# Block sums turned by VectorE instead of TensorE in a two-layer graph kernel, with another order of layer 0's loads and last work

## The chip, the cores and the metric

One core of a Trainium2 chip runs the kernel. The metric is the device time of one execution in microseconds (us). The five engines of the core are called by the profile's names: PE (TensorE; PEld is its weight load), DVE (VectorE), ACT (ScalarE), POOL (GpSimd) and SP (SyncE, which here only issues DMAs; SPq is its queue).

## The reference, cut to what matters

A graph with 3327 nodes and 128 features goes through two layers. Layer 0 is a graph convolution with batch norm; layer 1 is attention with 128 heads of width 8, whose logits get the adjacency matrix added twice.

```python
# layer 0
h = relu(layernorm(x))
deg = adj.sum(axis=1); deg = where(deg == 0, 1, deg)
agg = adj.T @ h / deg
h = agg @ W_n.T + b_n + h @ W_c.T + b_c
x = x + relu(gamma * (h - mean(h)) * rsqrt(var(h) + 1e-5) + beta)   # over nodes
# layer 1
h = relu(layernorm(x))
q, k, v = ((h @ W.T).reshape(128, 3327, 8) for W in (Wq, Wk, Wv))
a = einsum('dnh,dmh->dnm', q, k) * 128 ** -0.5 + adj + adj
out = einsum('dnm,dmh->dnh', softmax(a), v)
x = x + out.reshape(3327, 1024) @ Wo.T
```

## The kernel before, in words

All of it is one stream for each engine, in the order in which the program issues it; each engine works its stream in order, and waits where a tile that it needs isn't ready or a buffer isn't free.

**Layer 0** (from line 301). Nodes come in 26 chunks of 128. The features `xs` and all weights are loaded by DMAs on ACT's queue (L325 to L337), the adjacency rows `a`, one chunk of 1.66 MB after the other, on SP's (L431), with three buffers. `stats` and `normalise` (L345, L363) make the layer norm of all chunks ahead of the chunk loop. In the loop PE multiplies each chunk into seven banks `acc` (L433, 14 matmul records a chunk), ACT sums the rows of `a` (L437), DVE takes their largest value (L440), and `beside` and `spread` fit smaller matmuls in between: A turned, A times W_c, the norms of the weights, and the reciprocal degrees spread over partitions. Then `hidden` and the loop at L504 finish the convolution and its batch norm, with the last two `spread`s, `set_flag` (a bound that tells whether the plain exponentials are safe) and `weigh_early` in between. L570 to L617 make the residual, the second layer norm and its columns, project head group 0 to q, k, v, and write these and the columns `hd` to DRAM. SP and ACT load k, q and v back (L587 to L597), and POOL and ACT sort k's columns (L613).

**Attention** (from line 675). Heads are taken four at a time: 32 groups `i`, and in each the queries in 7 blocks `y` of `QB` = 476 columns (the last has 472), and in each block the 26 key chunks in 13 steps `s`. So there are 32 x 7 x 13 = 2912 steps. A step has four products (`product`, L750: two matmuls of 32 rows into one of three PSUM buffers). Three of them go through DVE, which adds the adjacency (`add`, L862), and then ACT takes one exponential of all three (`late`, L907). The fourth goes to ACT first (L871) and then to POOL, which multiplies it by exponentials of the adjacency that were made once and lie in DRAM (`weighted`, L874). In steps 3, 7 and 11 (`DOUBLE`) it is two and two. Three steps later (`LAG`) PE multiplies the exponentials by v, with a column of ones, into the block's bank `av` (`second`, `weigh`, L623): for each of the four heads, at partitions 32b to 32b + 8, eight sums and the divisor. Two banks take turns by block.

**The end of a block** (`finish`, L628) is a generator whose parts run inside the next block's steps, one part at each step in `PARTS` = 3, 5, 6, 7, 8. Step 3: DVE copies the sums to SBUF (L633). Steps 5 and 6: PE turns them, four matmuls of two records each against the identity, two in each step (L640), back into the bank. Step 7: DVE clamps and inverts the divisors and multiplies (L648, L649, L651). Step 8: SP stores the quotients to `att` (L658; L665 for the last rows). Into steps 7 and 11 the program also fits the projections of later head groups and the output product of the group before (`begin`, `go_on`; L208, L269, L279). SP loads the adjacency tiles `at` (four buffers) and the exponentials `wt` (three) two steps ahead (`fetch`, L734, L738), and q, k, v of the next group spread evenly over a group's steps (`loads`). q is loaded in four DMAs of 8 rows for each head and k in two of 16 rows, since each half of q and the whole of k stand twice in their 32 rows (L140, L148).

Of the kernel before, what the change touches and what calls it, by code (L numbers as in the profile page):

```python
# [20 lines left out]
H = 8  # L21
# [5 lines left out]
QB = 476  # L27
# [9 lines left out]
PARTS = (3, 5, 6, 7, 8)  # L37
# [9 lines left out]
def tile_two_layer_gnn(  # L47
# [42 lines left out]
    xd = dram.tile([NP, D], F32, name="xd")  # L90
# [47 lines left out]
    def q_loads(q, p0, d, n0=0, n=NP):  # L138

        qs = qT[:, bass.ds(d * N + n0, n)].rearrange("(a h) n -> a h n", h=H)  # L140
        return [
            (q[p0 + i * H : p0 + (i + 1) * H, n0 : n0 + n].bitcast(F32), qs[i // 2])
            for i in range(4)
        ]

    def k_loads(k, p0, d, n0, n):
        cols = bass.ds(d * N + n0, n)
        return [  # L148
            (k[p0 + i * 2 * H : p0 + (i + 1) * 2 * H].bitcast(F32), kT[:, cols])
            for i in range(2)  # L150
        ]
# [52 lines left out]
    def projection(wk, hj, j, s, e, quick, ov, factor):  # L204
# [8 lines left out]
        if s == 2:  # L213
# [5 lines left out]
            if e:  # L219
                nc.sync.dma_start(  # L220
# [3 lines left out]
        o = wk.tile([P, 2, NB], F32R, name="o")  # L224
        factor = 1.0 if s else factor
        if quick:
            nc.scalar.activation(o[:CH, 0], bank[:CH], AF.Copy, scale=factor)
            nc.vector.scalar_tensor_tensor(
                o[:CH, 1], bank[:CH], factor, o[:CH, 0].bitcast(F32), ALU.mult, ALU.subtract
            )  # L230
        else:
# [3 lines left out]
            else:  # L235
# [3 lines left out]
                o[:CH, 1], f[:CH], o[:CH, 0].bitcast(F32), ALU.subtract  # L239
            )  # L240
        yield
        for a in range(2):
            g = a * H + e * (H // 2)
            nc.sync.dma_start(
                (qT, kT)[s][g : g + H // 2, tok].rearrange("g (p u) -> p g u", u=D),
                o[:CH, a].bitcast(F32).rearrange("p (h u) -> p h u", u=D),
            )

    def projections(wk, hj, j, quick, ov, factor):
        return [  # L250
            projection(wk, hj, j, s, e, quick, ov, factor) for s in (1, 0, 2) for e in range(2)
        ]

    def outputs(wk, j):
# [7 lines left out]
        nc.sync.dma_start(xj[:CH], xd[j * CH : (j + 1) * CH, :])  # L262
# [38 lines left out]
    with tc.tile_pool(name="l0", bufs=1) as l0, tc.tile_pool(  # L301
        name="l0adj", bufs=3
    ) as ap, tc.tile_pool(name="l0s", bufs=2) as sp, tc.tile_pool(
# [18 lines left out]

        xr = x[: (NC - 1) * P, :].rearrange("(c p) d -> p c d", p=P)
        nc.vector.memset(xs[:, NC - 1, :], 0.0)
        for c0, c1 in ((0, 8), (8, NC - 1)):  # L325
            nc.scalar.dma_start(xs[:, c0:c1, :], xr[:, c0:c1, :])
        for p0, p1 in pieces(N - (NC - 1) * P):
            nc.scalar.dma_start(
                xs[p0:p1, NC - 1, :], x[(NC - 1) * P + p0 : (NC - 1) * P + p1, :]
            )  # L330
        nc.scalar.dma_start(wc, WcT)
        for i, b in enumerate((b_n, b_c, gamma, beta)):
            nc.scalar.dma_start(cols[:, i : i + 1], b.rearrange("o d -> d o"))
        nc.scalar.dma_start(wn, WnT)
        for t, w in zip(wqk, (WqT, WkT, WvT)):
# [781 lines left out]
```

## Time and profile before

| | |
|---|---|
| median of 3 runs | 10376.06 us (10374.61 to 10379.81) |
| the profiled execution | 10381.98 us, span of its instructions 10380.2 us |
| first adjacency matmul | 23.45 us after the start |
| first product of the attention (L750) | 261.67 us |
| first addition by DVE (L862) | 271.80 us |
| one head group in the middle | 313 us, 7 blocks |
| last exponential begins | 10353.66 us |
| TensorE clock granted, mean | 0.992 |

The attention is 97% of the time, and it repeats 32 times; what a step in it costs is multiplied by 2912, and what a block costs by 224. Busy shares in this profile are read with care: a matmul's end is modelled, so that PE seems busy while its result waits. The starts of ACT's instructions, one after another, tell more: an engine that begins the next instruction as soon as the one before it lets it isn't waiting. In an answer on time, a row is "start, duration, engine, line, operation, what is written and read, shape, count", and brackets at the end tell how long the engine stood idle before it and what ended that.

### The profile page before, as it was taken

How to read it: one execution, taken by the hardware profiler on the slowest of the kernel's cores; microseconds unless marked ns; L12 is line 12 of the kernel's file. 1: busy time of each engine (PE TensorE's matmuls, PEld its weight loads, DVE VectorE, ACT ScalarE, POOL GpSimd, SP SyncE). 2: the span in 40 equal slices, each digit the busy share in tenths (PEclk: the TensorE clock that was granted, in tenths of full speed). 3: DMA queues.
4: the chain of work that ended last, by engine and by line, in shares of the span. 5: the costliest groups of instructions: out<-in, count | busy, mean ns of one | idle time of the engine just before them, and what ended most of it. 6: DMA issues, size and time to landing. Idle time of an engine off the chain costs nothing. (4 is left out here: it accounts for less than half of the span.)

```text
span 10380.2 us, 189900 instructions
## 1 busy us (share of the span) xinstructions
PE 9995.3 (96%) x73327; PEld 3082.3 (30%) x73327; DVE 9366.9 (90%) x9533; ACT 9923.2 (96%) x6655; POOL 8439.0 (81%) x4317
## 2 busy tenths in 40 slices
PE   7899999999999999999999999999999999999999
PEld 3222222222222222222222222222222222222222
DVE  5789999999999999999999999999999999999998
ACT  4899999999999999999999999999999999999998
POOL 1678888888888888888888888888888888888887
PEclk9899999999999999999999999999999999999999
DMA  6766666666666666666665666666666665666554
GB/s 228 221 177 164 163 170 167 166 165 165 163 166 170 165 165 162 164 168 167 167 164 159 168 167 168 167 161 162 167 169 167 167 161 159 171 169 167 157 153 127
DMA packets 1114449, 1735.99 MB, mean 167 GB/s; under 512 B 194622, under 2 KB 1089980, under 8 KB 1105852
## 3 DMA queue, kind: packets, MB, share of 16 engines
q1 hardware_dynamic: 1108766, 1716.94, 60.9%
q8 instruction: 575, 9.42, 0.4%
q10 hardware_dynamic: 4350, 4.20, 0.1%
q14 instruction: 342, 2.80, 0.1%
q0 software_dynamic: 416, 2.63, 0.1%
HBM read 1621.05 MB, written 102.38 MB: 166 GB/s over the span
## 5 line engine op out<-in xcount | busy, mean ns | idle before, releaser
L862 DVE SCALAR_TENSOR_TENSOR d<-at,s 128x952 f32<-128x952 f32 x8064 | 8797.4, 1141 | 681.7 <-PE s L750 397.6
L874 POOL TENSOR_TENSOR f<-f,wt 128x952 f32<-128x952 f32 (+1 forms) x3584 | 7939.0, 2233 | 1674.3 <-ACT f L871 1649.9
L907 ACT ACTIVATE d<-d 128x2856 f32<-128x2856 f32 (+1 forms) x2912 | 7027.9, 2413 | 2.2 <-DVE d L862 1.9
L623 PE MATMUL av<-d,v 128*9 128x476 f32 x32256 | 5065.6, 566 | 0.7 <-ACT d L907 0.7
L750 PE MATMUL s<-q,k 32*128 32x476 f32 x23296 | 4087.3, 475 | 313.8 <-ACT f L871 243.5
L871 ACT ACTIVATE f<-s 128x952 f32<-128x952 f32 (+1 forms) x3584 | 3396.9, 970 | 281.8 <-PE s L750 266.0
L750 PEld LDWEIGHTS s<-q,k 32*128 32x128 f32 x23296 | 1739.5, 182 | 5500.2 <-DVE d L862 3005.9
L623 PE MATMUL av<-f,v 128*9 128x476 f32 x14336 | 2849.0, 566 | 0.0
L623 PEld LDWEIGHTS av<-d,v 128*9 128x9 f32 x32256 | 583.3, 88 | 1161.5 <-issue 1149.6
L640 PE MATMUL av<-ident,avs 128*119 128x36 f32 (+1 forms) x1792 | 474.1, 391 | 0.8 <-DVE avs L633 0.8
L640 PEld LDWEIGHTS av<-ident,avs 128*119 128x119 f32 (+1 forms) x1792 | 422.9, 308 | 103.1 <-issue 101.5
L623 PEld LDWEIGHTS av<-f,v 128*9 128x9 f32 x14336 | 316.6, 88 | 112.4 <-issue 88.7
L192 POOL CAST k<-ks 128x256 fp32r<-128x256 f32 x434 | 283.8, 654 | 0.0
L433 PE MATMUL acc<-a,A 128*128 128x512 f32 (+1 forms) x364 | 151.6, 569 | 24.2 <-ACT A L367 23.4
L238 POOL TENSOR_TENSOR o<-pf,o 104x512 fp32r<-104x512 f32 x124 | 160.0, 1291 | 9.9
L633 DVE COPY avs<-av 128x476 f32<-128x476 f32 (+1 forms) x224 | 145.4, 649 | 4.6 <-PE av L623 4.6
L440 DVE TENSOR_REDUCE amax<-a 128x1 f32<-128x3327 f32 x26 | 93.7, 3611 | 36.4 <-DMA a<-in_adj 36.4
L433 PEld LDWEIGHTS acc<-a,A 128*128 128x128 f32 x364 | 69.0, 192 | 109.0 <-issue 84.5
L236 DVE TENSOR_SCALAR pf<-av,low_half 104x512 f32<-104x512 f32 x62 | 46.6, 751 | 46.8 <-PE av L208 46.6
L406 POOL TENSOR_TENSOR sq<-wk 128x512 f32<-128x512 f32 x2 | 2.1, 1042 | 102.5 <-PE aside L407 102.5
L234 DVE COPY pf<-av 104x512 f32<-104x512 f32 x62 | 42.9, 692 | 46.9 <-PE av L208 46.9
L437 ACT ACTIVATE junk<-a 128x3327 bf16<-128x3327 f32 x26 | 77.5, 2979 | 7.1 <-DMA a<-in_adj 6.8
(123 smaller groups left out, 1032.3 us busy)
## 6 DMA issues: line engine op xcount, KB each, us to landing
at<-in_adjT SPq DMA_DIRECT2D x1728, 476.0 KB
wt<-wd SPq DMA_DIRECT2D x1536, 238.0 KB
at<-in_adjT SPq DMA_DIRECT2D x288, 472.0 KB
wt<-wd SPq DMA_DIRECT2D x256, 236.0 KB
ks<-kT SPq DMA_DIRECT2D x496, 104.0 KB
q<-qT SPq DMA_DIRECT2D x496, 104.0 KB
a<-in_adj SPq DMA_DIRECT2D x26, 1663.5 KB
kT<-o SPq DMA_DIRECT2D x128, 208.0 KB
```

What stands on the lines that cost most here:

```text
L192: nc.gpsimd.tensor_copy(k[:, c : c + n, half * 64 : half * 64 + 64], ks.bitcast(F32).rearrange("g (p c) -> g c p", c=NC)[:, c : c + n, :],)
L238: nc.gpsimd.tensor_tensor(o[:CH, 1], f[:CH], o[:CH, 0].bitcast(F32), ALU.subtract)
L433: nc.tensor.matmul(acc[i][:, :w], A[:, c, :], a[:, n0 : n0 + w], start=(c == 0), stop=(c == NC - 1),)
L440: nc.vector.tensor_reduce(amax[:, c : c + 1], a[:, :N], AX.X, ALU.max, apply_absolute_value=True)
L623: nc.tensor.matmul(av[32 * b : 32 * b + H + 1, :w], tiles[2][:, b, c, :], e, start=first, stop=last,)
L633: nc.vector.tensor_copy(avs[:, : R * J], av[:, : R * J])
L640: nc.tensor.matmul(pt[:R, j, :], avs[:, j : j + (R - 1) * J + 1 : J], some, start=True, stop=True)
L750: nc.tensor.matmul(p[:, x, :we], k[rs, c, :], q[rs, n0 : n0 + we], start=True, stop=True,)
L862: nc.vector.scalar_tensor_tensor(d[:, j, :, :w], have[0, i, y, c // 2][:, c % 2, :w] .unsqueeze(1).to_broadcast([P, 2, w]), SAFE / 2, p[:, ...
L871: nc.scalar.activation(f[:, :, :w], p[:, :, :w], AF.Exp, scale=2.0)
L874: nc.gpsimd.tensor_tensor(f[:, :, :w], f[:, :, :w], have[1, i, y, c][:, :w].unsqueeze(1).to_broadcast([P, 2, w]), ALU.mult,)
L907: nc.scalar.activation(flat, flat, AF.Exp, scale=2.0)
```

## The change

- `finish`: DVE turns the sums itself, in 32 x 32 squares, reading the bank and writing `avs` in SBUF; the four matmuls go. The block is taken as 32 runs of J columns (15, or 14 in the last block), so `QB` becomes 480 and the last block 448, and 32 J is the block's width. The reciprocals are written into J spare columns of the block's bank, from column 480. `PARTS` loses steps 5 and 6. The store to `att` is one DMA for each of the four heads, 32 rows of 480 bytes, and in the last block of a group two for each.
- q and k loads: one DMA for what stood in two, with the source repeated by a stride of zero: q two DMAs for each head, k one. Half as many are issued.
- Layer 0: the features come on SP's queue, the first four chunks ahead of the first adjacency chunk and the rest between the next ones; q, k, v and output weights follow between later chunks; small weights move to POOL's queue; ACT takes its square root once at the start. The layer norm is made chunk group by chunk group in the chunk loop. In the last chunk the flag and the last `spread` are made between the matmuls.
- From layer 0 to the attention: projections of group 0 are spread over the residual work, with their stores on three queues; `hd` is written in two parts, `xd` once in another layout (read back in one or two DMAs); the first loads of k, q, v and the sorting of k move into the attention, behind its first `at` and `wt` loads, all on SP; the pools of the attention are laid out in another order.

```diff
-QB = 476
+QB = 480
-PARTS = (3, 5, 6, 7, 8)
+PARTS = (3, 7, 8)
-            (q[p0 + i * H : p0 + (i + 1) * H, n0 : n0 + n].bitcast(F32), qs[i // 2])
-            for i in range(4)
+            (
+                q[p0 + a * 2 * H : p0 + (a + 1) * 2 * H, n0 : n0 + n].bitcast(F32),
+                qs[a].unsqueeze(0).to_broadcast([2, H, n]),
+            )
+            for a in range(2)
         ]
     def k_loads(k, p0, d, n0, n):
-        cols = bass.ds(d * N + n0, n)
-        return [
-            (k[p0 + i * 2 * H : p0 + (i + 1) * 2 * H].bitcast(F32), kT[:, cols])
-            for i in range(2)
-        ]
+        ks = kT[:, bass.ds(d * N + n0, n)]
+        return [(
+            k[p0 : p0 + 4 * H].bitcast(F32), ks.unsqueeze(0).to_broadcast([2, 2 * H, n])
+        )]
...
-        nc.sync.dma_start(xj[:CH], xd[j * CH : (j + 1) * CH, :])
+        for c in range(j * CH // P, ((j + 1) * CH - 1) // P + 1):
+            m0, m1 = max(j * CH, c * P), min((j + 1) * CH, (c + 1) * P)
+            nc.sync.dma_start(
+                xj[m0 - j * CH : m1 - j * CH], xd[m0 - c * P : m1 - c * P, c, :]
+            )
...
+        nc.sync.dma_start(xs[:, :4, :], xr[:, :4, :])
+        tiles = []
+
+        def load(c):
+
+            a = ap.tile([P, 7 * NB], F32, name="a")
+            nc.sync.dma_start(a[:, :N], adj[c * P : (c + 1) * P, :])
+            tiles.append(a)
+            if c in (1, 2):
+                c0, c1 = (4, 14) if c == 1 else (14, NC - 1)
+                nc.sync.dma_start(xs[:, c0:c1, :], xr[:, c0:c1, :])
+            if c == 2:
+                for p0, p1 in pieces(N - (NC - 1) * P):
+                    nc.sync.dma_start(
+                        xs[p0:p1, NC - 1, :], x[(NC - 1) * P + p0 : (NC - 1) * P + p1, :]
+                    )
+            if c in (5, 7, 9):
+                i = (c - 5) // 2
+                nc.sync.dma_start(wqk[i], (WqT, WkT, WvT)[i])
+            if c == 11:
+                nc.sync.dma_start(wo, WoT.rearrange("(e p) o -> p e o", p=P))
+
+
+        root = l0.tile([P, 1], F32, name="root")
+        nc.scalar.activation(root, eps, AF.Sqrt)
+        nc.gpsimd.dma_start(wc, WcT)
         for i, b in enumerate((b_n, b_c, gamma, beta)):
-            nc.scalar.dma_start(cols[:, i : i + 1], b.rearrange("o d -> d o"))
-        nc.scalar.dma_start(wn, WnT)
-        for t, w in zip(wqk, (WqT, WkT, WvT)):
-            nc.scalar.dma_start(t, w)
-        nc.scalar.dma_start(wo, WoT.rearrange("(e p) o -> p e o", p=P))
+            nc.gpsimd.dma_start(cols[:, i : i + 1], b.rearrange("o d -> d o"))
+        nc.gpsimd.dma_start(wn, WnT)
...
-        stats(0)
-        for i in range(NQ):
-            if i + 1 < NQ:
-                stats(i + 1)
-            normalise(i, A)
-        nc.vector.tensor_add(bias, cols[:, 0:1], cols[:, 1:2])
...
+        load(0)
+        for c in range(NC):
+            a = tiles[c]
+            if c + 1 < NC:
+                load(c + 1)
+            if c < NQ:
+                if c == 0:
+                    stats(c)
+                normalise(c, A)
+                if c + 1 < NQ:
+                    stats(c + 1)
+
+            def gather(i0, i1):
+                for i, (n0, w) in list(enumerate(blocks))[i0:i1]:
+                    nc.tensor.matmul(
+                        acc[i][:, :w], A[:, c, :], a[:, n0 : n0 + w],
+                        start=(c == 0), stop=(c == NC - 1),
+                    )
+
+            last = c == NC - 1
+            gather(0, 4 if last else len(blocks))
+            nc.scalar.activation(
+                junk, a[:, :N], AF.Copy, accum_out=deg[:, c : c + 1]
+            )
+            nc.vector.tensor_reduce(
+                amax[:, c : c + 1], a[:, :N], AX.X, ALU.max, apply_absolute_value=True
+            )
+            if last:
+                nc.vector.tensor_reduce(top, amax, AX.X, ALU.max)
+                flags = set_flag()
+                next(flags)
+                gather(4, len(blocks))
+                next(flags)
+                spreading = spread(NQ - 1)
+                next(spreading)
+            if c >= 1:
+                beside(c - 1)
+            if c - 1 == 2 * NQ + 4:
+                set_bound()
+
+            i = c - 2 * NQ - 5
+            if 0 <= i < NQ - 1 and 4 * i + 4 <= c:
+                for _ in spread(i):
+                    pass
...
@@ -507,11 +560,9 @@
             nc.tensor.matmul(acc[i][:, :w], wn, B2[:, s], start=True, stop=True)
             if i >= 1:
                 hidden(i - 1)
-            if i in (0, 2):
-                spread(NQ - 2 + i // 2)
-            if i == 3:
-                set_flag()
-            if i in (4, 6):
+            if i == 0:
+                next(spreading)
+            if i in (0, 1):
                 weigh_early()
...
+        now = projections(
+            sp, B2[:, :CH], 0, True, ov, low_half[:CH, 1:2], (nc.scalar, nc.sync, nc.gpsimd)
+        )
+        banks = [acc[i] for i in (6, 5, 4, 0)] + [aside, acc[1]]
+
+        def multiply(*js):
+            for j in js:
+                drive(now[j], banks[j])
+
+        def project(*js):
+            for j in js:
+                drive(now[j])
+                drive(now[j])
+
+        multiply(0, 1)
+        project(0, 1)
         residual(2)
-        project_now(0, [acc[j] for j in (6, 5, 4, 0)] + [aside, acc[1]])
-
-        q, k, v = sets[0]
-        ks = sets[1][1].rearrange("p c n -> p (c n)")
-        for b in range(G):
-            for args in k_loads(ks, 32 * b, b, 0, NP):
-                nc.sync.dma_start(*args)
-        for args in v_loads(v, 0):
-            nc.sync.dma_start(*args)
+        multiply(2, 3)
+        relu(4)
+        stats(2, False)
+        project(2, 3)
+        residual(3)
+        multiply(4, 5)
+        relu(5)
+        stats(3, False)
+        relu(6)
+        project(4, 5)
         for i in range(4, NQ):
-            relu(i)
-
-        for b in range(G):
-            for args in q_loads(q, 32 * b, b, 0, NB):
-                nc.scalar.dma_start(*args)
-        for i in range(2, NQ):
-            if i > 2:
...
     def finish(rp, av, d0, n0, w):
-        J = 4
-        R = -(-w // J)
-        avs = rp.tile([P, QB], F32, name="avs")
-        nc.vector.tensor_copy(avs[:, : R * J], av[:, : R * J])
-        yield
-
-        pt = av[:, : J * G * (H + 1)].rearrange("p (j q) -> p j q", j=J)
-
-        some = ident.rearrange("p (b h) -> p b h", h=32)[:, :, : H + 1]
-        for j in range(J):
-            nc.tensor.matmul(
-                pt[:R, j, :], avs[:, j : j + (R - 1) * J + 1 : J], some, start=True, stop=True
-            )
-            if j % 2:
-                yield
-        pv = pt.rearrange("p j (b h) -> p b j h", h=H + 1)
-        ri = rp.tile([P, G, J], F32, name="ri")
-
-        nc.vector.tensor_scalar(ri[:R], pv[:R, :, :, H], 1e-30, None, ALU.max)
-        nc.vector.reciprocal(ri[:R], ri[:R])
-        o = rp.tile([P, G, J, H], F32, name="oq")
-        nc.vector.tensor_tensor(
-            o[:R], pv[:R, :, :, :H], ri[:R].unsqueeze(3).to_broadcast([R, G, J, H]),
-            ALU.mult,
+        J = -(-w // 32)
+
+        avs = rp.tile([P, QB // 32, 32], F32, name="avs")
+        nc.vector.transpose(
+            avs[:, :J, :].rearrange("p j h -> p (j h)"),
+            av[:, : 32 * J].rearrange("p (q j) -> p j q", j=J),
         )
         yield
-        r, j = divmod(min(w, N - n0), J)
-        nc.sync.dma_start(
-            attb[bass.ds(d0, G), n0 : n0 + r * J, :].rearrange(
-                "b (p j) h -> p b (j h)", j=J
-            ),
-            o[:r].rearrange("p b j h -> p b (j h)"),
+        ri = av[:, QB : QB + J]
+
+        nc.vector.tensor_scalar(ri, avs[:, :J, H], 1e-30, None, ALU.max)
+        nc.vector.reciprocal(ri, ri)
+        o = rp.tile([P, QB // 32, H], F32, name="oq")
+        nc.vector.tensor_tensor(
+            o[:, :J, :], avs[:, :J, :H], ri.unsqueeze(2).to_broadcast([P, J, H]), ALU.mult
         )
-        if j:
-            nc.sync.dma_start(
-                attb[bass.ds(d0, G), n0 + r * J : n0 + r * J + j, :].rearrange(
-                    "b (o j) h -> o b (j h)", o=1
-                ),
-                o[r : r + 1, :, :j, :].rearrange("p b j h -> p b (j h)"),
+        yield
+
+        r = 32 - (n0 + 32 * J > N)
+        for b in range(G):
+            ab = att[bass.ds((d0 + b if b else d0) * N + n0, 32 * J), :].rearrange(
+                "(q j) h -> q (j h)", j=J
             )
+            ob = o[32 * b : 32 * b + 32, :J, :].rearrange("q j h -> q (j h)")
+            nc.sync.dma_start(ab[:r], ob[:r])
+            if r < 32:
+                nc.sync.dma_start(ab[r:, : (J - 1) * H], ob[r:, : (J - 1) * H])
...
+        with tc.tile_pool(name="exd", bufs=4) as ep, tc.tile_pool(
+            name="adj", bufs=4
+        ) as ap, tc.tile_pool(name="adw", bufs=3) as wp, tc.tile_pool(
             name="exf", bufs=6
-        ) as fp, tc.tile_pool(name="exd", bufs=4) as ep, tc.tile_pool(
-            name="res", bufs=2
-        ) as rp, tc.tile_pool(name="psc", bufs=3, space=PSUM) as psc, tc.tile_pool(
+        ) as fp, tc.tile_pool(name="res", bufs=2) as rp, tc.tile_pool(
+            name="wk", bufs=2
+        ) as wk, tc.tile_pool(name="psc", bufs=3, space=PSUM) as psc, tc.tile_pool(
             name="pav", bufs=1, space=PSUM
         ) as pav:
@@ -835,6 +870,34 @@
                     i, y, s = steps[x]
                     return product(i, y, *pairs(s)[1][0])
+                def first_loads():
+
+                    q, k, v = sets[0]
+                    ks = sets[1][1].rearrange("p c n -> p (c n)")
+                    for b in range(G):
+                        for args in k_loads(ks, 32 * b, b, 0, NP):
+                            nc.sync.dma_start(*args)
+
+                    for b in range(G):
+                        for args in q_loads(q, 32 * b, b, 0, NB):
+                            nc.sync.dma_start(*args)
+                    for args in v_loads(v, 0):
+                        nc.sync.dma_start(*args)
+
+                    for c, copy in (
+                        (16, nc.scalar.copy), (0, nc.vector.tensor_copy),
+                        (4, nc.gpsimd.tensor_copy), (8, nc.scalar.copy),
+                        (20, nc.vector.tensor_copy), (12, nc.gpsimd.tensor_copy),
+                        (24, nc.vector.tensor_copy),
+                    ):
+                        n = min(4, NC - c)
+                        copy(
+                            k[:, c : c + n, :],
+                            ks.bitcast(F32).rearrange("g (p c) -> g c p", c=NC)[:, c : c + n, :],
+                        )
+
+                fetch(PRE - 1)
+                first_loads()
```

## The prediction

> **What bounds the kernel now.** I read the page first, for the groups that repeat in the attention, then the stages in windows, then ACT's own rows in order of time through one block, and last all engines around the two places where ACT stood idle.
>
> ```profile
> PE 9995.3 (96%) x73327; PEld 3082.3 (30%) x73327; DVE 9366.9 (90%) x9533; ACT 9923.2 (96%) x6655; POOL 8439.0 (81%) x4317
> ...
> L907 ACT ACTIVATE d<-d 128x2856 f32<-128x2856 f32 (+1 forms) x2912 | 7027.9, 2413 | 2.2 <-DVE d L862 1.9
> ...
> L640 PE MATMUL av<-ident,avs 128*119 128x36 f32 (+1 forms) x1792 | 474.1, 391 | 0.8 <-DVE avs L633 0.8
> ...
> L633 DVE COPY avs<-av 128x476 f32<-128x476 f32 (+1 forms) x224 | 145.4, 649 | 4.6 <-PE av L623 4.6
> ```
>
> PE and ACT look equally full. One head group in the middle (columns: window, length, then PE, PEld, DVE, ACT, POOL busy, clock, DMA share, GB/s) says the same:
>
> ```profile
> 5000.00:5313.00 313.00, 304.90 (x2280) 93.22 (x2276) 287.86 (x291) 305.38 (x204) 263.22 (x135) 1.00 0.61 165
> ```
>
> ACT is idle for 7.6 of 313 us, and PE's busy share is no proof that PE is the limit, because ends of matmuls are modelled. The order of ACT's rows decides it:
>
> ```profile
> 5043.09 2.63 ACT L907 ACTIVATE d<-d 128x2856 f32<-128x2856 f32 x1
> 5045.57 1.86 ACT L871 ACTIVATE f<-s 128x952 f32<-128x952 f32 x2
> 5047.26 1.85 ACT L907 ACTIVATE d<-d 128x1904 f32<-128x1904 f32 x1
> 5048.94 1.02 ACT L871 ACTIVATE f<-s 128x952 f32<-128x952 f32 x1
> 5049.78 2.65 ACT L907 ACTIVATE d<-d 128x2856 f32<-128x2856 f32 x1
> 5053.04 0.97 ACT L871 ACTIVATE f<-s 128x952 f32<-128x952 f32 x1 [0.60 <-PE s L750]
> 5053.90 2.58 ACT L907 ACTIVATE d<-d 128x2856 f32<-128x2856 f32 x1
> 5056.96 0.97 ACT L871 ACTIVATE f<-s 128x952 f32<-128x952 f32 x1 [0.47 <-PE s L750]
> 5057.82 2.58 ACT L907 ACTIVATE d<-d 128x2856 f32<-128x2856 f32 x1
> ```
>
> Without brackets a row starts before the one ahead of it has ended: ACT sets the pace. A plain step, L907 to L907, takes 3.33 us; only two steps of a block are longer, 5049.78 to 5053.90 (4.12) and 5053.90 to 5057.82 (3.92). All seven blocks of the window show the pair, means 4.09 and 3.91, and every other step is ACT's 3.33, those with projections too. What PE does there:
>
> ```profile
> 5050.14 0.49 PE L750 MATMUL s<-q,k 32*128 32x476 f32 x4
> 5050.56 1.05 PE L640 MATMUL av<-ident,avs 128*118 128x36 f32 x4
> ...
> 5052.46 0.49 PE L750 MATMUL s<-q,k 32*128 32x476 f32 x4
> ...
> 5053.04 0.97 ACT L871 ACTIVATE f<-s 128x952 f32<-128x952 f32 x1 [0.60 <-PE s L750]
> ```
>
> The turning matmuls hold PE for about 1 us in the middle of a step. A step of PE without them is 2.66 us (half steps from 5007.89 to 5009.22, 1.33 apart), with them 3.66, over ACT's 3.33, twice in a row, with three product buffers as the only cushion. So the bound is ACT, and PE takes over in two steps of thirteen.
>
> The start has another limit, the layer norm's input and ACT's queue:
>
> ```profile
> 2.31 12.04 ACTq L328 DMA_DIRECT2D xs<-in_x  x2
> 13.57 0.88 DVE L348 BATCH_NORM_STATS2 ln_st<-xs 128x6 f32<-128x128 f32 x4 [12.13 <-DMA xs<-in_x]
> 20.86 1.28 ACT L355 ACT_TABLE_LOAD   x1 [19.46 <-DMA cols<-in_beta]
> 23.45 1.22 PE L433 MATMUL acc<-a,A 128*128 128x512 f32 x1 [23.45 <-ACT A L367]
> ```
>
> Features land at 13.57; ACT, busy issuing loads, takes its first root at 22, and PE begins at 23.45.
>
> [...]
>
> **The change, part by part.** I sum against the profiled execution (span 10380.2, time 10382.0) and take the difference off the median 10376.1; the two stand 0.06% apart.
>
> *Turning (finish).* Goes: 8 PE records a block in steps 5 and 6. ACT's excess there is (4.09 - 3.33) + (3.91 - 3.33) = 1.34 us a block. If ACT then runs through, 224 x 1.34 = 300 us. What is late next? Needs of a block of 13 steps: ACT 44.7 - 1.34 = 43.4. DVE 36 additions at 1.09 (13 in 14.22 us in a back-to-back stretch) = 39.4, plus 0.65 copy, 0.71 quotients and about 1.0 for projections: 41.7. POOL 16 products at 2.23 plus 2.4 for sorting and projections: 38.1. PE 13 x 2.66 = 34.6 and some 2 for projections. ACT stays the bound, DVE has 1.7 us left.
>
> *Turning on DVE.* Comes: one transpose of 128 x 480 in place of the 0.65 us copy, at the same place in step 3, where DVE has only two additions (2.2 of 3.4 us). Lower bound: the copy's price, 476 elements in 0.65 us[...]. [...] I take 0.66. The three quotient operations go from 119 x 16 to 128 x 15 lanes, with 0.17, 0.25 and 0.29 us as before; that they write to the bank costs nothing that a row shows. QB = 480: six blocks of 480 and one of 448 instead of 476 and 472 have the same 3328 columns and the same instruction count, so ACT's sum stays.
>
> *Stores and SP.* Three more stores a block at 0.32 us (row L658) are 1.0 us; in a group's last block up to 4 us more (0.65 for each odd one, row L665). Sixteen q and k issues fewer a group, at some 0.37, give 6 back. Behind them on SP stand `at` and `wt` loads, waited for by DVE and POOL. SP waits 155 of 313 us for POOL to free `wt` buffers, so that is covered: 0.
>
> *Repeated-source loads.* Bytes stay, engines may not. Many engines: 0. Two engines: the fastest window of layer 0 moved 420 GB/s, 26 for each engine, so a load of 2 x 104 KB takes 4.05 us on its two engines instead of about 1, 16 times a group, and an `at` or `wt` load issued behind it lands some 4 us later. `wt` has three buffers, one issue every 5.6 us, so a load has some 11 us from issue to use, less 4 for landing: 7 are left. Hidden, 0, in the long run. [...]
>
> *Start.* The first four chunks (256 KB) and adjacency chunk 0 (1.66 MB) at 420 GB/s need 4.6 us, plus some 3 until the first bytes: 7 to 9. ACT's root is out of the way. First matmul at 8.5 instead of 23.45: 15 us. From there PE is the limit (14 records 5.74 us and one more product, 6.0 to 6.4 a chunk, no idle), and a chunk's load needs 4.0, so the gain holds to the end of the loop, less 1.0 for one more `spread` in it: -14.
>
> *Last work of layer 0.* From the first L506 (190.83) to the first relu (215.15): 24.3 us. DVE's chain alone is 7 x (0.67 + 0.69 + 0.69) less overlap, 13, and 3 for the batch norm. The flag and the last `spread`, now made beside matmuls, leave it: -8.
>
> *To the attention.* From the first relu to the first addition: 56.7 us before (271.80 - 215.15). k's stores land about 16 us in. Many engines: the four k loads and sorting end at some 34, the tiles under the exponentials are free at 33: gain 21. Two engines: 4 x 425 KB at 52 GB/s is 32 us, q 5 more: 57, no gain, and the later q columns (eight loads of 3.4 us) hold `at` loads up in the first block, at most +15. I take 0 between -21 and +15.
>
> Sum: -300 - 14 - 8 + 0 = -322, so 10376 - 322 = 10054.
>
> **The rivals.**
> - *Forecast*: ACT runs through; 10015 to 10090, by the open crossing, the turn's price and a little more in the first blocks (there the stalls were 3.06 and 2.39).
> - *Half*: another wait takes part of the place. DVE is the candidate: 41.7 of 43.4, nearly full in steps 7 to 10, and PE waits for it at L862 more than for anything (3005.9 us). For: little slack. Against: blocks with projections show no ACT gap now. If half of the 300 comes: 10204.
> - *Slower*: loads on two engines stall the attention. Place: every q and k load, 31 x 16 = 496; price: the part of its 4.05 us that outlasts the buffers; it decides from 322 / 496 = 0.65 us each. With 1 us each: 10054 + 496 = 10550. [...] Against: 7 us of cushion.
> - *Not as said*: the turn is spread over other engines' slack but changes nothing. Excluded by the pair of long steps standing exactly where L640 runs, in all seven blocks.
>
> **How the numbers follow.** Forecast 0.74, half (10090 to 10330) 0.13, slower 0.11, no change 0.02. A measurement of this kernel tells about 0.2% (21 us) from none. Forecast and half are both faster: 0.87; same 0.02; slower 0.11. Range: the forecast's own with its lower end at 10010 for both startup gains in full, and up to 10190 for the greater part of the half case.
>
> **What would show it.** Right: no L640; ACT's rows of steps 5 and 6 3.33 apart without brackets; a head group of 303 to 304 us; a DVE transpose near 0.66 us; first L433 at 7 to 10; first L862 at 235 to 255. Wrong: brackets on ACT from DVE or DMAs in other steps; POOL waiting for k's DMA at L192 or for `wt`; a transpose over 1.9 us, which would put DVE's block over ACT's.

## The result

The changed kernel takes 10237.35 us (median of 4 runs, 10224.43 to 10253.06) beside 10377.93 us for the kernel before (4 runs, 10374.61 to 10380.59). The ratio is 0.9865, 95% interval 0.9847 to 0.9884: faster by 1.35%, where 3.1% were forecast. The time lies 183 us over the forecast and 47 us over the range. The profiled execution took 10253.06 us, its span is 10251.3, and the mean granted clock is 0.981.

The page of the changed kernel, the busy line and the groups that answer to those of before (group lines: line, engine, operation, tiles, count, then busy us and mean ns, then idle time ahead of them and what ended it):

```profile
PE 9787.2 (95%) x71535; PEld 2720.9 (27%) x71535; DVE 9306.6 (91%) x9527; ACT 9886.6 (96%) x6662; POOL 8434.3 (82%) x4325
...
L970 ACT ACTIVATE d<-d 128x2880 f32<-128x2880 f32 (+1 forms) x2912 | 7071.3, 2428 | 97.0 <-DVE d L925 95.8
...
L680 DVE STREAM_TRANSPOSE avs<-av 128x480 f32<-128x480 f32 (+1 forms) x224 | 149.5, 667 | 4.4 <-PE av L670 4.4
```

The turning matmuls are gone, and the transpose costs what the copy did. But ACT, which was idle for 2.2 us ahead of its large exponential, is now idle for 97.0. The waits (engine, line, releaser: us in total, times, longest) say who is late first:

```profile
POOL f L937 <- DMA wt<-wd: 200.6, 57, 10.6
...
DVE d L925 <- DMA at<-in_adjT: 136.7, 98, 11.3
...
ACT d L970 <- DVE d L925: 95.8, 99, 2.7
...
ACT f L934 <- PE s L785: 48.4, 29, 2.6
```

Before, POOL waited 3.2 us in all for `wt`, and DVE 1.6 us for `at`. The old wait of ACT for the products has fallen from 266.0 to 48.4 us, as meant, and late adjacency loads have come in. ACT's rows in order of time behind the double step 3 of a block, where the two long steps stood before, in a stretch that no late load disturbs:

```profile
5087.51 1.81 ACT L970 ACTIVATE d<-d 128x1920 f32<-128x1920 f32 x1
5089.21 0.97 ACT L934 ACTIVATE f<-s 128x960 f32<-128x960 f32 x1
5090.06 2.61 ACT L970 ACTIVATE d<-d 128x2880 f32<-128x2880 f32 x1
5092.55 0.98 ACT L934 ACTIVATE f<-s 128x960 f32<-128x960 f32 x1
5093.40 2.63 ACT L970 ACTIVATE d<-d 128x2880 f32<-128x2880 f32 x1
5095.90 0.99 ACT L934 ACTIVATE f<-s 128x960 f32<-128x960 f32 x1
5096.75 2.63 ACT L970 ACTIVATE d<-d 128x2880 f32<-128x2880 f32 x1
```

Steps 3.34 and 3.35 apart, no bracket: the pair of long steps is gone. Some 70 us earlier, all engines in order of time at one stall:

```profile
5018.14 0.65 SPq L172 DMA_DIRECT2D ks<-kT  x1
...
5024.33 0.62 POOL L240 CAST o<-pf 104x512 fp32r<-104x512 f32 x1
...
5024.98 1.69 SPq L247 DMA_DIRECT2D kT<-o  x2
...
5026.77 0.41 SPq L773 DMA_DIRECT2D at<-in_adjT  x1
...
5027.22 1.66 SPq L769 DMA_DIRECT2D wt<-wd  x2
5028.98 0.38 SPq L773 DMA_DIRECT2D at<-in_adjT  x1
5029.79 1.53 SPq L172 DMA_DIRECT2D v<-v  x1
...
5036.01 3.28 DVE L925 SCALAR_TENSOR_TENSOR d<-at,s 128x960 f32<-128x960 f32 x3 [2.00 <-DMA at<-in_adjT]
...
5037.01 4.44 POOL L937 TENSOR_TENSOR f<-f,wt 128x960 f32<-128x960 f32 x2 [4.07 <-DMA wt<-wd]
...
5037.26 2.61 ACT L970 ACTIVATE d<-d 128x2880 f32<-128x2880 f32 x1 [1.66 <-DVE d L925]
```

Read it from the top. SP issues the fourth load of k at 5018.14 and then nothing until 5024.98: the next item in its stream is the store of a projection (L247), and that waits for POOL to make `o` (L240, 5024.33), which POOL does only after the products ahead of it. Then two `at`, two `wt` and a load of v are issued within 4 us. DVE, POOL and, through DVE, ACT are then idle until 5036 to 5037.

That the repeated sources run on two engines is seen where nothing else is under way, at the start of the attention (window, length, PE, PEld, DVE, ACT, POOL busy, clock, DMA share, GB/s):

```profile
235.00:240.00 5.00, 0.00 (x0) 0.00 (x0) 0.00 (x0) 0.00 (x0) 0.00 (x0) 0.50 0.13 54
240.00:245.00 5.00, 0.00 (x0) 0.00 (x0) 0.00 (x0) 0.00 (x0) 0.00 (x0) 0.50 0.12 53
```

A share of 0.125 of 16 engines is what two busy engines make, at 53 GB/s together, or 26 each, as many as one of 16 moved in the fastest window of layer 0 before (420 / 16). In the kernel whose only difference is the old loads (the first experiment), the stretch in which k is loaded reads:

```profile
220.00:225.00 5.00, 4.05 (x17) 3.37 (x18) 3.27 (x11) 4.71 (x10) 3.85 (x8) 0.50 1.04 146
225.00:230.00 5.00, 0.94 (x7) 0.70 (x5) 1.40 (x3) 1.19 (x2) 1.68 (x3) 0.84 0.92 134
```

The share there, 1.04 and 0.92, is that of all 16 engines, and the rate, 146 and 134 GB/s, is about 2.6 times as high.

By the stretches of the program, from the issues of the reads of `att` (L262, one for each group), the first read comes at 799.59 us instead of 783.43 (+16.2), 31 group periods take 9433.6 instead of 9580.4 (-146.9), the end +1.8: -128.9. A group is no longer 313 us each time, but scatters from 305 to 314 (the last three periods, at the end of the program, left out).

### The profile page after: what moved, and what is told of

It reads as the page before. It is cut to its first block, busy times and chain, and to the rows that moved or that the text cites. A ratio compares the mean times of both kernels' runs of the same rounds, so it can differ in the third digit from the quotient of the medians.

```text
span 10251.3 us, 186610 instructions
## 1 busy us (share of the span) xinstructions
PE 9787.2 (95%) x71535; PEld 2720.9 (27%) x71535; DVE 9306.6 (91%) x9527; ACT 9886.6 (96%) x6662; POOL 8434.3 (82%) x4325
## 3 DMA queue, kind: packets, MB, share of 16 engines
q0 software_dynamic: 784, 4.03, 0.1%
## 4 chain that ended last, share of the span: by engine, by line
POOL 30%; PE 25%; ACT 20%; issue 11%; DMA 11%; DVE 2%; SPq 1%; POOLq 0%; ACTq 0%; DVEq 0%
POOL f L937 29%; PE av L670 13%; ACT f L934 11%; PE s L785 9%; ACT d L970 9%; DMA at<-in_adjT 6%; DMA wt<-wd 2%; DVE d L925 2%; PE acc L502 1%; DMA t<-in_adjT 1%; PE av L210 1%; POOL k L194 1%; DMA q<-qT 1%; POOL o L241 1%; POOL o L240 0%
## 5 line engine op out<-in xcount | busy, mean ns | idle before, releaser
L925 DVE SCALAR_TENSOR_TENSOR d<-at,s 128x960 f32<-128x960 f32 x8064 | 8733.3, 1138 | 632.9 <-PE s L785 361.2
L937 POOL TENSOR_TENSOR f<-f,wt 128x960 f32<-128x960 f32 (+1 forms) x3584 | 7933.3, 2233 | 1552.2 <-ACT f L934 1322.0
L970 ACT ACTIVATE d<-d 128x2880 f32<-128x2880 f32 (+1 forms) x2912 | 7071.3, 2428 | 97.0 <-DVE d L925 95.8
L670 PE MATMUL av<-d,v 128*9 128x480 f32 x32256 | 5126.0, 573 | 0.6 <-ACT d L970 0.6
L785 PE MATMUL s<-q,k 32*128 32x480 f32 x23296 | 4267.6, 479 | 412.8 <-ACT f L934 179.9
L934 ACT ACTIVATE f<-s 128x960 f32<-128x960 f32 (+1 forms) x3584 | 3443.7, 987 | 54.7 <-PE s L785 48.4
L785 PEld LDWEIGHTS s<-q,k 32*128 32x128 f32 x23296 | 1801.2, 183 | 5745.0 <-DVE d L925 3710.2
L670 PE MATMUL av<-f,v 128*9 128x480 f32 x14336 | 2876.7, 570 | 0.0
L680 DVE STREAM_TRANSPOSE avs<-av 128x480 f32<-128x480 f32 (+1 forms) x224 | 149.5, 667 | 4.4 <-PE av L670 4.4
L240 POOL CAST o<-pf 104x512 fp32r<-104x512 f32 x124 | 76.1, 613 | 0.0
```

What stands on the lines that cost most here:

```text
L670: nc.tensor.matmul(av[32 * b : 32 * b + H + 1, :w], tiles[2][:, b, c, :], e, start=first, stop=last,)
L680: nc.vector.transpose(avs[:, :J, :].rearrange("p j h -> p (j h)"), av[:, : 32 * J].rearrange("p (q j) -> p j q", j=J),)
L785: nc.tensor.matmul(p[:, x, :we], k[rs, c, :], q[rs, n0 : n0 + we], start=True, stop=True,)
L925: nc.vector.scalar_tensor_tensor(d[:, j, :, :w], have[0, i, y, c // 2][:, c % 2, :w] .unsqueeze(1).to_broadcast([P, 2, w]), SAFE / 2, p[:, ...
L934: nc.scalar.activation(f[:, :, :w], p[:, :, :w], AF.Exp, scale=2.0)
L937: nc.gpsimd.tensor_tensor(f[:, :, :w], f[:, :, :w], have[1, i, y, c][:, :w].unsqueeze(1).to_broadcast([P, 2, w]), ALU.mult,)
```

## The experiments

Theory: everything but the repeated sources does what was forecast, and these lose some 180 us. Rivals: DVE's turn takes part of its gain back; layer 0 and the crossing from it to the attention lose it. Each experiment ran beside the kernel before, whose medians were 10374.6 to 10377.4. "First read" is the first read of `att`, "a group" the mean over the 31 periods that follow it; both come from the one profiled execution of each kernel, the times from medians.

| kernel | time, us | ratio (95%) | first read | a group, against old loads |
|---|---|---|---|---|
| changed | 10237.35 | 0.9865 (0.9847-0.9884) | 799.6 | +4.24 |
| e1: old loads | 10068.39 | 0.9703 (0.9687-0.9719) | 742.9 | 0 |
| e3: turn alone | 10084.76 | 0.9719 (0.9703-0.9735) | 765.6 | -0.06 |
| e4: repeated loads alone | 10547.25 | 1.0166 (1.0149-1.0183) | 827.1 | +3.96 (against the kernel before) |
| e5: q alone repeated | 10101.36 | 0.9734 (0.9718-0.9750) | 775.6 | +0.15 |
| e6: k alone repeated | 10208.18 | 0.9840 (0.9823-0.9856) | 783.1 | +3.41 |
| e8: group 0 alone repeated | 10105.52 | 0.9741 (0.9725-0.9757) | 783.2 | 0.00 |
| e7: k's loads spread | 10167.93 | 0.9804 (0.9788-0.9821) | 794.3 | +1.69 |
| e9: v behind the second k | 10287.74 | 0.9918 (0.9902-0.9935) | 812.4 | +4.85 |
| e10: v before k | 10144.49 | 0.9776 (0.9760-0.9792) | 792.7 | +0.97 |
| e11: loads two blocks later | 10123.47 | 0.9758 (0.9742-0.9775) | 793.2 | +0.36 |
| e12: stores by POOL | 10096.61 | 0.9732 (0.9716-0.9749) | 771.9 | +0.19 |
| e13: e1 and stores by POOL | 10046.12 | 0.9681 (0.9668-0.9695) | 725.4 | +0.21 |

The profiled execution of the changed kernel is the slowest of its four (10253.06 us, the median is 10237.35), and that of e1 the fastest (10064.53, median 10068.39). So +4.24 is on the high side: the medians of the two lie 169.0 us apart, the profiled spans 188.5. Differences of 0.2 us a group are within what the runs of one kernel differ by (6 us of time in e1, 10 in e13).

### Which part loses the time

**e1**, the changed kernel with the loads of before:

```diff
-            (
-                q[p0 + a * 2 * H : p0 + (a + 1) * 2 * H, n0 : n0 + n].bitcast(F32),
-                qs[a].unsqueeze(0).to_broadcast([2, H, n]),
-            )
-            for a in range(2)
+            (q[p0 + i * H : p0 + (i + 1) * H, n0 : n0 + n].bitcast(F32), qs[i // 2])
+            for i in range(4)
...
-        ks = kT[:, bass.ds(d * N + n0, n)]
-        return [(
-            k[p0 : p0 + 4 * H].bitcast(F32), ks.unsqueeze(0).to_broadcast([2, 2 * H, n])
-        )]
+        cols = bass.ds(d * N + n0, n)
+        return [
+            (k[p0 + i * 2 * H : p0 + (i + 1) * 2 * H].bitcast(F32), kT[:, cols])
+            for i in range(2)
+        ]
```

> The changed kernel with q and k loaded as before: four plain DMAs of 8 rows for a head's q, two of 16 rows for its k. Theory (the loads with a repeated source run on two DMA engines and hold up the loads behind them): the head group falls from 308.5 us to between 303.5 and 305, DVE's and POOL's waits for at and wt loads nearly vanish, the first product of the attention comes at about 235 instead of 263 us, the whole takes 10030 to 10075 us. Rival (DVE has become nearly the bound with its turn in the block, and three or seven more stores a block sit in SP's queue): the group stays at 307 to 309, the whole within 40 us of the changed kernel's 10237 less the 30 us of the start.

**e3**, the kernel before with the new `finish`, `QB` = 480 and `PARTS` = (3, 7, 8), and nothing else:

> The kernel before with the new end of a block alone (DVE turns the sums, blocks of 480, four stores), its old loads and old layer 0. Theory: 1.34 us for each of 224 blocks, so the group goes from 312.9 to 303.5 to 304.5 us and the whole to 10070 to 10090. Rival (the turn itself gives only half, since DVE or the stores take over): 10200 to 10240.

**e4**, the kernel before with the two repeated-source functions, and nothing else:

> The kernel before with the loads of repeated source alone. Theory of two engines: the attention starts 20 to 40 us later and each group loses 1 to 5 us, less than in the changed kernel because PE's turning gives the loads more time; 10430 to 10560 us. Rival (these loads cost nothing, half as many issues): 10365 to 10390.

The span of e1 is 10062.8, and the forecast's sum on the profiled span was 10380.2 - 322 = 10058. Its groups take 303.6 to 304.5 us, the last three left out. The turn alone takes 298.5 us off the span (10380.2 to 10081.7) where 300 were forecast. The repeated loads alone make the kernel before slower by 1.66%. So the loss is theirs, in both kernels; the rivals fall. One head group of e1 (window columns as above), where the changed kernel has ACT busy for 309.48 of 313:

```profile
5000.00:5313.00 313.00, 304.91 (x2296) 84.49 (x2292) 295.19 (x299) 312.84 (x209) 271.65 (x139) 1.00 0.64 174
```

Between the profiled executions of e1 and the changed kernel lie 188.5 us of span: 56.7 up to the first read, 131.5 in the 31 periods, 0.3 at the end.

### q or k, start or groups

**e5**, the changed kernel with k's loads as before and q's repeated; **e6**, the other way round; **e8**, repeated sources in group 0's loads only (`first_loads` and `others`), and in `loads`, for groups 1 to 31, the functions of before as `q_old` and `k_old`:

```diff
-        qs = [dma(*a) for b in range(G) for a in q_loads(q, 32 * b, batch(b))]
+        qs = [dma(*a) for b in range(G) for a in q_old(q, 32 * b, batch(b))]
...
-                    for a in k_loads(ks, 32 * b, batch(b), half * (NP // 2), NP // 2)
+                    for a in k_old(ks, 32 * b, batch(b), half * (NP // 2), NP // 2)
```

> The changed kernel with k loaded as before and q with a repeated source. Both have the same bytes in a group. Theory of two engines: about half of the loss in the groups stays (306 us a group), the start loses the 32 us of the k loads; 10110 to 10160 us. If k's loads alone matter, because POOL's sorting waits for them: 10040 to 10080. If q's alone: near 10200.

> The changed kernel with q's loads as before and only k's from a source repeated for both halves. Theory (k's loads alone carry the stalls, since they stand four in a row in the order, one about every 8.4 us, and each holds two of the sixteen DMA engines for 4.05 us, 0.48 of their time on top of the 0.60 to 0.65 that all sixteen are busy): the groups keep about 308 us, and the time is the changed kernel's 10237 less q's part at the start, some 30 us: about 10205 (10190 to 10225). Rival (only q's and k's repeated loads together are too much; each alone is hidden): groups of about 304, time about 10095.

> The changed kernel with the repeated sources only in the loads of group 0 (the first loads and the rest of its q); the loads of groups 1 to 31 as before. Theory (start and groups are two separate costs): groups of 303.7 to 304.2; the first read of att late by what the start alone makes, 25 to 57 us behind the 742.85 of the kernel with all old loads; time about 10095 to 10125. Rival (the delay up to the first read of att comes from the loads for group 1, which fall before it): the first read of att within 30 us of 742.85 and the time about 10095; with the theory's upper end all of the 57 us belongs to group 0's own loads.

Two separate costs. In the groups k's loads make nearly all of it (+3.41 of +4.24), q's, with the same bytes and a repeated source as well, nothing to speak of (+0.15). At the start group 0's own loads make 40 of the 57 us (e8), and group 1's, which fall before the first read, by difference the rest. The rival for e6, that only both together are too much, falls, and so does that for e8. The theory for e5 was wrong: half of the groups' loss was to stay with q's loads, and almost none did.

### Why k's loads stall and q's don't

POOL's waits of over 1 us for `wt` in the changed kernel stand at two places of a group: behind the four loads of k's first half, where v's follow (115.8 us in 27 cases after the first read), and at the first loads of q after those (55.6 us in 24). The four identical loads of k's second half, some 170 us later, are followed by none, though they stand closer: 22.7 us from the first issue to the fourth on average, in the first half 29.6. Rate or place?

The program's planner keeps a group's 33 loads and sortings in a list and spreads them over the group's steps; an entry is called a turn. **e7**: each load of k is followed by another turn, so that they come half as often:

```diff
-            todo += vv if half == 0 else []
+                todo += vv[b : b + 1] if half == 0 else [lambda: None]
```

(the new line stands inside the loop over `b`).

> The changed kernel, all repeated sources kept, but in the planner's list each of the four loads of k is followed by another turn: by one of the loads of v in the first half, by an empty turn in the second; so one k load about every 15 us instead of every 8 us. Theory (it is the rate at which repeated loads follow each other on two engines that stalls the attention, not their bytes or number): most of the 4.6 us a group goes, groups of 304 to 306, time about 10120 to 10170. Rival (every repeated load of k costs its stall, wherever it stands, by SP's waits for its semaphore or by the copies of k behind the last of them): groups stay at 308, time within 15 us of the changed kernel's 10237.

A group lost 1.69 us instead of 4.24, and the time fell into the theory's interval. Taken alone this would have settled on the rate, wrongly, as e11 shows: spreading also moves the loads.

**e9** puts v's loads behind the second half's k, **e10** ahead of the first half's:

```diff
-            todo += vv if half == 0 else []
+            todo += vv if half == 1 else []
```

> The changed kernel with all its repeated sources; in the planner's list the three loads of v stand behind the second half's four loads of k instead of behind the first half's. In the changed kernel the stalls come where v's loads follow k's, and none comes at the second half's k, where no v follows. Theory (two engines are behind after four k loads close together, and v's large loads on top of that make the attention's own loads late): the stall moves with v to the second half, groups keep 306 to 309 us, time 10200 to 10240. Rival (the stall needs what is particular to the first half, the stores of the projections ahead of and between its k loads): it stays there or, without v, shrinks; groups of at most 306, time about 10150.

> The changed kernel with all its repeated sources; in the planner's list the three loads of v stand ahead of the first half's four loads of k, and the first two loads of q directly behind those. Theory (v's large loads behind k's make the stall): without them behind k's, groups of 304 to 306, time 10110 to 10165. Rival (whatever stands behind four repeated loads of k is late, q's repeated loads most of all): groups of 307 to 310, time 10210 to 10260.

Both outcomes of e9 were missed. The stall didn't move with v: between 5000 and 6300 us the second half, with v behind it, has none, and in the first half it now hits q's loads behind k's, a little harder (+4.85). e10's time fell into the interval of the same theory, that v's loads behind k's make the stall, which e9 had just refuted: moving v also shifts k's loads. In e10 four loads of k with two of q directly behind cost 0.97. So neither v's size nor what follows k decides. What differs is when the loads meet the two stores of `kT`. In e10 three of the four loads of k are issued after the second store, in the changed kernel none (5024.98 in the rows above, the fourth load at 5018.14).

**e11** moves all loads of the next group two blocks on, away from the stores of `kT`, which makes them follow each other faster (by the planner's formula one turn each 1.7 steps instead of 2.5):

```diff
-    FROM = [3 * SU] + [LAG + 1] * (NG - 1)
+    FROM = [3 * SU] + [LAG + 1 + 2 * SU] * (NG - 1)
```

> The changed kernel with all its repeated sources; the loads of the next group begin two blocks later in a group (FROM plus 2 SU), so that the first half's four loads of k no longer stand among the stores of kT; the planner then has 53 steps instead of 79 for the same 33 turns, one load about every 5 to 6 us instead of every 8. Theory (the place decides: k's repeated loads stall only where they meet the stores of the projections on SP): groups of at most 306 us, time 10110 to 10180. Rival (the rate decides: 4.05 us on two engines every 5.4 us is 0.75 of their time on top of the 0.6 that all are busy): groups of 312 us or more, time over 10330.

**e12** leaves every load in its place and has POOL issue the projections' stores, behind its own copies:

```diff
-                        extra.extend(projections(wk, hj, j, False, ov, low_half[:CH, 1:2]))
+                        extra.extend(
+                            projections(wk, hj, j, False, ov, low_half[:CH, 1:2], (nc.gpsimd,) * 3)
+                        )
```

> The changed kernel with all its repeated sources; the stores of the projections for groups 1 to 31 are issued by POOL, behind its own copies, instead of by SP, so SP is no longer held where it waits for POOL to have made o, and the loads behind are no longer bunched; the bytes and the order of loads stay. Theory (SP's being held between k's loads is half of the cause): groups of 303.7 to 306, time 10090 to 10180. Rival (the two engines' own backlog and the bytes of stores and v are enough): groups of 307 to 310, time 10200 to 10260.

Both go the theory's way, far from the rivals. In e11 loads of k were 4.6 to 10.5 us apart (5016.98, 5027.47, 5032.04, 5038.74), and a group still costs only 0.36: the mean rate isn't it. Not every late load has gone in e11. POOL still waits 103.0 us for `wt` (200.6 in the changed kernel), but DVE only 24.5 us for `at` (136.7), and it is through DVE that ACT is reached. In e12 the repeated loads are the same, and a group costs 0.19. SP's waits in the changed kernel, of which the first two are gone in e12:

```profile
SPq L247 <- POOL o L240: 511.4, 123, 6.6
...
SPq L247 <- POOL o L241: 116.3, 124, 1.0
...
SPq L773 <- DMA ks<-kT: 75.1, 57, 3.1
```

The first two make 627.7 us in which all loads behind a projection's store stood still. In the third, SP waits until a load of k has landed before it issues the next `at`; e12 keeps 24.0 us of it. This hold isn't the cause by itself: in e11 SP waits 90.6 us at L773 and 79.9 us at L769 for loads of k, and the group hardly suffers. With POOL issuing (e12), the waits that stalled the groups, and the head group:

```profile
DVE d L927 <- DMA at<-in_adjT: 25.7, 11, 10.6
...
POOL f L939 <- DMA wt<-wd: 10.5, 1, 10.5
```

```profile
5000.00:5313.00 313.00, 304.33 (x2290) 84.30 (x2282) 294.67 (x299) 313.00 (x210) 278.94 (x148) 1.00 0.61 172
```

ACT is busy for all 313 us. Nor is it the holding alone, for e1 keeps it and loses nothing:

```profile
SPq L245 <- POOL o L238: 564.1, 124, 7.2
```

So the stall of the groups needs both: k's loads with a repeated source, for about 4 us each on two engines (an estimate from the 53 GB/s at the start), and the projections' stores on SP among them. It goes when either is taken away (e1, e12) and nearly goes when the two are moved apart (e11). That the harm in the stores is SP's being held, for up to 6.6 us, is what the rows at the stall show, but e12 doesn't prove it alone: with POOL issuing, the stores also go through another queue (in e13, whose stores POOL issues as well, q0 moves 71.82 MB, in the changed kernel 4.03), and the kernel's DMAs make 949595 packets instead of 1035806. A store by SP that isn't held wasn't tried.

### The version that beats both

**e13** is e1 with e12's stores.

> The changed kernel with q's and k's loads as before and, besides, the stores of the projections for groups 1 to 31 issued by POOL. Theory (with loads on many engines nothing is late in the groups even where SP is held, so only the first groups can gain): groups of 303.7 to 304 as in the kernel with old loads alone, the first read of att up to 11 us earlier than 742.85 there, time 10057 to 10069. Rival (POOL's 0.8 us for each store, some 7 us a group, costs time): groups of 305 or more, time over 10100.

10046.12 us, 3.2% under the kernel before. Under e1 it lies 22 us, but the two ran at different times on different chips and the intervals of their ratios overlap, so this lead isn't certain. The groups stay as in e1 within 0.2 us (POOL is busy for 8639.3 us instead of 8437.6, the price of issuing the stores: 248 issues at L245 of 0.80 to 0.82 us, 200.1 us in all), and the first read comes at 725.4 instead of 742.9, so the gain over e1 is at the start, and larger than the 11 us expected. Of those 17.5 us, 3.5 were there before the first addition already, where the edit issues nothing yet.

## Why the prediction was wrong

*Turning.* Right in mechanism and size: 298.5 us of span instead of 300 (e3), groups of 303.6 to 304.5 in e1 where 303 to 304 were forecast. The transpose takes 667 ns at the forecast's 0.66. That the turn would cost about what the copy did was the author's estimate, since no row of before shows a transpose; measured, 480 four-byte elements a partition are turned in 667 ns (L680), where 476 were copied in 649 (L633 before). The rival "half" did not occur: with old loads ACT waits 2.0 us in all for DVE at L968.

*Start and last work of layer 0.* Right. The first adjacency matmul begins at 8.66 us (forecast 8.5), the first relu at 193.88 (about 193).

*To the attention.* Both bounds were too low. From the first relu to the first addition e1 takes 47.4 us where many engines were to give some 36, the changed kernel 72.3 where two engines were to give 57. The 32 us for k's four loads were right: 1.70 MB at 53 GB/s. But q's and the rest came behind them, since SP, too, was held while k's loads were under way: at L883 it waited 20.1 us for loads of k. The eight issues of q in the changed kernel and the sixteen in e1:

```profile
217.53 41.53 SPq L883 DMA_DIRECT2D q<-qT  x8
```

```profile
221.42 15.26 SPq L881 DMA_DIRECT2D q<-qT  x16
```

From the first addition to the first read it took 533.5 us instead of e1's 500.3. The forecast allowed 15 us for all of that. It is in part luck, then, that e1's span comes so near to the forecast's sum: that sum has 0 for this stretch, while for loads on many engines, which e1 has, the forecast's own figure was a gain of 21.

*Issues.* The forecast expected half as many issues to give back 6 us a group. They gave back about 1.7: the issue of a repeated load takes 0.64 us, of an old one 0.42 (k) or 0.33 (q).

*Repeated-source loads: the step that failed.* "7 are left. Hidden, 0, in the long run." Two engines were one of the forecast's two cases, an estimate that no row of before shows; the share of 0.12 to 0.13 in the windows from 235 to 245 us agrees with it. Which two they are, and whether they are the same for each load, no row shows; where the expectations of e6 and e11 reckon what k's loads take of "their time", that they are the same was an assumption. The price of one load was right too, as an estimate from the same windows: at 53 GB/s its 208 KB take 4.0 us. The cushion was wrong: it was worked out as if SP issued each `wt` and `at` load as soon as its buffer came free. The forecast itself had listed SP's waits and put them down as cover ("SP waits 155 of 313 us for POOL to free `wt` buffers, so that is covered: 0."). Another wait of SP's, for POOL's `o` at each projection's store, takes from the same cushion. It was there to be read in the trace of before, among SP's waits in the same 313 us:

```profile
SPq L734 <- POOL f L874: 155.3, 49, 5.7
...
SPq L244 <- POOL o L237: 21.6, 4, 6.3
```

In the changed kernel it is 4.2 us in the mean (511.4 / 123), 6.2 in the case shown. With a load's 4.05 this is, as an estimate, 8 to 10 us, more than the 7 that were left. The term put at 0 measured 188.5 us of span, 131.5 in the groups and 56.7 up to the first read. By the medians it is 169.0 of the 183 by which the forecast missed; the other 14 are what e1 lies over it.

*The rival "slower"* had this very mechanism and place, at a price for each of the 16 loads of a group and a turning point of 0.65 us. The loads cost 4.24 / 16 = 0.27 us each on average, and not evenly: q's nothing, k's second half nothing. The kernel before, without the turn's gain, shows what it looks like alone: +1.66%.

Open: why q's repeated loads, some of which meet the stores of `qT`, cost only 0.15 us a group, and why e9 costs more than the changed kernel. Nor is it separated whether POOL's queue helps only by freeing SP's order or also because its stores come at other moments, through another queue and in fewer packets. Of the start's 56.7 us, 29 remain in e12; 22.5 of these lie in the crossing (first addition at 265.08 us, in e1 at 242.59), where nothing hides the 32 us of k's loads.

## What to carry to other kernels

Fewer DMAs aren't cheaper DMAs (here half as many issues gave back about 1.7 us a group, and the repeated sources still cost 4.24): before two loads are folded into one by a repeated source, look at how many DMA engines the new pattern takes, in a window in which nothing else is moved. Work out a load's cushion from the stream of the engine that issues it, with every other wait in that stream, above all stores that wait for a busy engine; two delays that are each hidden alone can fail together (here 4.05 and 4.2 to 6.2 us, as an estimate, against 7). And spread or reorder experiments move things in time as well: one that confirms a rate needs its counterpart with the rate raised and the place changed.

## What wasn't expected of the hardware

In this kernel the granted clock falls behind a stall. In stretches of 8 us around the one shown (clock in the column before the DMA share):

```profile
5016.00:5024.00 8.00, 7.97 (x56) 2.11 (x56) 7.15 (x8) 8.00 (x6) 7.52 (x4) 1.00 0.78 220
5024.00:5032.00 8.00, 7.96 (x66) 1.90 (x58) 7.83 (x9) 8.00 (x6) 7.92 (x6) 1.00 0.73 185
5032.00:5040.00 8.00, 6.25 (x44) 1.60 (x40) 5.88 (x6) 6.34 (x5) 3.93 (x3) 0.81 1.06 284
5040.00:5048.00 8.00, 8.00 (x56) 1.86 (x56) 6.18 (x6) 7.06 (x6) 8.00 (x4) 0.76 0.50 149
```

PE is idle for 1.75 us between 5032 and 5040, the clock is 0.81 and then 0.76, and ACT is still not full in the last row. These two are means over stretches in which the clock was halved for a while:

```profile
5037.10:5043.80 6.70, 6.58 (x34) 1.47 (x38) 4.87 (x6) 6.48 (x5) 6.70 (x4) 0.50 0.72 202
```

Between 800 and 10000 us the clock records of the changed kernel hold 25 such drops to 0.50, of 3.4 to 10.2 us and 177 us together; at 24 of them PE had been idle for 0.8 to 2.8 us without a break, at most 4.5 us earlier. In e1 and in the kernel before there is no such drop in this stretch. The DMA columns of the third row, a share of 1.06 and 284 GB/s, fit the loads that were held back coming all together. In the means the clock is 0.981 for the changed kernel and 0.994 for e1. How much of a stall's cost is the clock's wasn't separated.
